# Layer 0's attention by joined head pairs: two of three pairs take all sixteen score groups first, then their values, and every row sum goes through DRAM

## The chip, the cores and the metric

The kernel runs on one core of one Trainium2 chip, as one launch. The metric is the device time of that launch in microseconds, lower is better. A core has a matrix engine (TensorE, PE in the profile), a vector engine (VectorE, DVE), a scalar engine for activations and copies (ScalarE, ACT), GpSimd (POOL), and SyncE (SP), which here only issues transfers. Each takes its instructions in the order in which the program holds them.

## The reference, cut to what matters

Eight images of 32 x 32 pixels with 384 channels pass through two layers in float32. Layer 0, the one that is changed, is a group norm and then attention with relative positions over all 1024 pixels of an image, six heads of 64 channels:

```python
qkv = x.reshape(b, hw, c) @ qkv_w + qkv_b                 # hw = 1024, c = 384
attn = jnp.einsum('bqd,bkd->bqk', q * SCALE, k)           # 1024 x 1024 per head
attn = attn + rel_h[..., :, None] + rel_w[..., None, :]   # from q and tables of offsets
out = jnp.einsum('bqk,bkd->bqd', jax.nn.softmax(attn), v)
x = x + out @ proj_w + proj_b
```

Layer 1 is a layer norm, causal attention with one head of 384, added to its input, and a second layer norm with a feed-forward of 1536 whose weights are binarized and whose activations are quantized in groups of one image; its groups cover the first five images, for the last three it yields zero. So images 0 to 4 run the feed-forward, 5 to 7 don't.

## The kernel before, in words

One program text is run over the images in the order 5, 0, 1, 2, 3, 4, 6, 7 (`ORDER`). Image 5, the first, also carries the preparation of weights in its attention and has some branches of its own ("image one"). The path described is the fast one, `f`. Its softmax has no maximum taken off; at the end a flag says whether a sum went out of bounds, and if so a second, general path `g` runs everything again behind a branch.

Within an image: products make queries, keys and values (L578), the tables of relative positions are spread through DRAM (`spread`, L769, and `place`, L784 to L800), then come layer 0's attention (`attend0_fast`, L888), the projection (L1021, L524) added to the residual (L1029), the layer norm's statistics (L481 to L489) and the normed tokens `f_xn` (L494), their transposes on TensorE (`f_pt`, L431) with ScalarE's copies out (L432), the split forms for the next products (L588), layer 1's attention (L1199, L1213) and, for five images, the feed-forward (L1357, L1407), beside which the next image's group norm is prepared.

The attention goes over three pairs of heads (`p`), and within each over two halves of 512 queries (`half`):

- `scores(p, c, half)` for eight blocks `c` of 128 keys: two matmuls of keys by queries (L904), two that add the position rows from `r` (L908), one pair each for the two heads of the pair, which lie on the two halves of the partitions; then two exponentials on ScalarE (L915) into a page. A page is a 128 x 1024 tile of float32; there are twelve. [...]
- `add_up`: VectorE adds the eight pages (L920 once, L922 six times).
- `values`: sixteen matmuls (L930), two for each page, into one PSUM bank; ScalarE copies the result to `oT` (L1002).
- `over_tiles`: a transpose in blocks (L939) and a reduction (L941) fold the sum to `few`, 128 x 32.
- `gathered`: SP puts `few` to DRAM (L949) and gets it back in four pieces as `parts` (L953), so that each partition holds the sums of its own queries. `reciprocals` adds these up (L969) and inverts (L971); `widened` copies them wide (L978) and transposes (L979); POOL multiplies `oT` by it (L999). This is done a half later, behind that half's sixth add.
- The last half of an image (`last`) goes another way: its `few` goes through two small matmuls with a fold matrix (L964) instead, and VectorE multiplies both of the last pair's halves (L1012, L1015) in front of the projection.

`later(p + 1)` is called in the first half of a pair and makes the next pair's rows of positions: ScalarE rounds (L784), VectorE subtracts (L794), and sixteen transfers, eight issued by SP and eight by POOL, place them (L800). `residual` loads the image again (L122) and POOL adds the projection's bias to it (L883, eight instructions).

A scheduler keeps each engine's order close to the program's text. Where a helper named `behind_of` or `issue_after` is used, the instruction is held behind a named other one; on TensorE the whole chain of matmuls of the attention is written out that way (`last_matmul`). Pools give out tiles in turn: a page, or one of ten image-sized rooms (`image`, `flat`), is handed out again when its last reader is done.

The projection begins with its first four blocks of tokens in this order, so that the third head pair's part (k = 2) comes as late as possible:

```python
for j, ks in ((0, (0, 1)), (1, (0, 1)), (0, (2,)), (1, (2,)), (2, (0, 1, 2)), (3, (0, 1, 2))):
```

At the end, the last image's layer 1 attention holds one block back, judges the sums (L282 to L291) and adds; SP writes the last outputs (L1525), and every engine loads the flag (L1539) and branches on it (L1540).

## Time and profile before

| what | us |
|---|---|
| three runs of the kernel before | 2262.17, 2261.61, 2261.36 |
| their median | 2261.61 |
| the profiled execution's own time | 2262.38 |
| its span in the profile | 2260.7 |
| TensorE busy | 2251.2 |
| VectorE busy | 1613.0 |
| ScalarE busy | 1208.5 |
| POOL busy | 526.9 |
| L904, L908 and L930 on TensorE, layer 0's attention | 399.0 + 307.7 + 340.2 |
| L920 and L922, VectorE's adds | 63.6 + 366.6 |

The profiled execution takes 2262.38 us, of which 2260.7 are the span from the first to the last instruction, and it is 0.8 us over the median of the three plain runs. The granted clock of TensorE was 0.999 throughout. A line of a timeline gives the start in microseconds from the span's beginning, the duration, the engine, the line of the kernel, the operation, what it writes and reads, and how many were merged into the line; in square brackets stands the idle time of the engine just ahead, and what ended it. A float32 matmul shows as two records. Busy time is added up without overlaps. `DVEq` and `SPq` are the queues in front of an engine.

### The profile page before, as it was taken

The numbers are of one execution on the slowest core, as the hardware profiler recorded it, in microseconds if no ns is written. First come the engines' busy times: TensorE is split into PE (matmuls) and PEld (weight loads), VectorE is DVE, ScalarE is ACT, GpSimd is POOL, SyncE is SP. The second block draws the span as 40 slices with busy tenths as digits, with TensorE's granted clock in tenths as the row PEclk, the third lists the DMA queues.
The fourth block names the chain that finished last, engine by engine and source line by source line (L and its number), as shares of the span: only waits on it lengthen the run. The fifth ranks groups of instructions, "written<-read, shape, count | busy, mean of one in ns | idle before, by whom it ended". The sixth has DMA issues, their size and how long they took to land.

```text
span 2260.7 us, 30149 instructions
## 1 busy us (share of the span) xinstructions
PE 2251.2 (100%) x10597; PEld 1380.3 (61%) x10597; DVE 1613.0 (71%) x2746; ACT 1208.5 (53%) x2181; POOL 526.9 (23%) x696
## 2 busy tenths in 40 slices
PE   9999999999999999999999999999999999999998
PEld 4547554768546677547685475874477754755475
DVE  6888578876788548886468884578854778727882
ACT  4654266337664457654477543767444766317541
POOL 7513231230231301313102313013040131221310
PEclk9999999999999999999999999999999999999999
DMA  7520562130730205520318203064102382016200
GB/s 188 158 86 29 162 138 68 49 148 29 155 100 29 84 29 126 129 58 1 112 39 189 56 29 112 24 148 112 30 9 104 71 173 64 7 47 155 55 1 30
DMA packets 182049, 188.50 MB, mean 83 GB/s; under 512 B 138764, under 2 KB 151489, under 8 KB 179073
## 3 DMA queue, kind: packets, MB, share of 16 engines
q1 hardware_dynamic: 163680, 115.80, 21.1%
q0 software_dynamic: 17376, 69.30, 9.8%
q8 instruction: 87, 1.43, 0.3%
q10 hardware_dynamic: 832, 1.38, 0.2%
q14 instruction: 74, 0.60, 0.1%
HBM read 84.52 MB, written 51.56 MB: 60 GB/s over the span
## 4 chain that ended last, share of the span: by engine, by line
PE 99%; DMA 0%; DVE 0%; SPq 0%; issue 0%
PE f_s L904 15%; PE f_av L930 15%; PE f_av L1213 8%; PE f_s L1199 8%; PE f_y L1407 7%; PE f_y L1357 7%; PE f_qk L578 6%; PE f_s L908 4%; PE f_pr_A L578 4%; PE f_pr_B L578 3%; PE f_pj L1021 3%; PE f_pj L524 3%; PE f_rel L578 2%; PE f_pr_1v_A L578 2%; PE f_pr_1q_A L578 2%; PE f_pr_1v_B L578 2%
## 5 line engine op out<-in xcount | busy, mean ns | idle before, releaser
L915 ACT ACTIVATE f_pr<-f_s 128x512 f32<-128x512 f32 x768 | 412.5, 595 | 41.8 <-PE f_s L908 37.1
L904 PE MATMUL f_s<-f_q,f_k 64*128 64x512 f32 x1536 | 399.0, 595 | 0.0
L922 DVE TENSOR_TENSOR f_sum<-f_sum,f_pr 128x1024 f32<-128x1024 f32 x288 | 366.6, 1273 | 25.9
L930 PE MATMUL f_av<-f_pr,f_v 128*64 128x512 f32 x1536 | 340.2, 595 | 0.0
L908 PE MATMUL f_s<-f_r,unit 64*128 64x512 f32 x768 | 307.7, 792 | 0.0
L930 PEld LDWEIGHTS f_av<-f_pr,f_v 128*64 128x64 f32 x1536 | 106.0, 137 | 218.2 <-issue 191.9
L904 PEld LDWEIGHTS f_s<-f_q,f_k 64*128 64x128 f32 x1536 | 145.6, 186 | 124.4 <-issue 66.2
L1199 PE MATMUL f_s<-f_q,f_lnT 128*128 128x512 f32 (+3 forms) x576 | 198.3, 488 | 0.0
L1213 PE MATMUL f_av<-f_v,f_pr 128*128 128x385 f32 (+1 forms) x576 | 195.4, 486 | 0.0
L800 POOL DMA_DIRECT2D f_r<-f_far x192 | 102.0, 534 | 382.0 <-DVE f_far L794 174.4
L1208 ACT ACTIVATE f_pr<-f_s 128x512 f32<-128x512 f32 (+3 forms) x96 | 47.0, 490 | 203.2 <-DVE f_s L1204 160.3
L1213 PEld LDWEIGHTS f_av<-f_v,f_pr 128*128 128x128 f32 x576 | 108.1, 190 | 77.0 <-issue 11.5
L1199 PEld LDWEIGHTS f_s<-f_q,f_lnT 128*128 128x128 f32 x576 | 100.7, 190 | 70.0 <-issue 46.9
L1368 DVE TENSOR_REDUCE am<-f_h 128x1 f32<-128x1024 f32 (+2 forms) x80 | 71.6, 946 | 95.6 <-ACT f_h L1361 95.6
L1361 ACT ACTIVATE f_h<-f_y,biases 128x256 f32<-128x256 f32 x240 | 100.6, 470 | 67.0 <-PE f_y L1357 67.0
L908 PEld LDWEIGHTS f_s<-f_r,unit 64*128 64x128 f32 x768 | 75.0, 187 | 89.9 <-issue 89.4
L578 PE MATMUL f_qk<-f_gnT,wq_sb 128*128 128x512 f32 x288 | 127.9, 595 | 0.0
L1407 PE MATMUL f_y<-f_w2a,f_hilo 128*128 128x384 f32 x640 | 127.2, 341 | 0.0
L1002 ACT COPY f_oT<-f_av 128x512 f32<-128x512 f32 x40 | 23.4, 585 | 190.2 <-PE f_av L930 190.2
L920 DVE TENSOR_TENSOR f_sum<-f_pr,f_pr 128x1024 f32<-128x1024 f32 x48 | 63.6, 1325 | 73.5 <-ACT f_pr L915 73.5
L1407 PEld LDWEIGHTS f_y<-f_w2a,f_hilo 128*128 128x128 f32 x640 | 112.6, 188 | 3.8 <-issue 1.4
L1311 POOL PARTITION_ALL_REDUCE qa<-qg x10 | 3.7, 365 | 459.1 <-DVE qg L1309 459.1
(286 smaller groups left out, 4154.4 us busy)
## 6 DMA issues: line engine op xcount, KB each, us to landing
f_far<-f_far SPq DMA_DIRECT2D x48, 512.0 KB, 5.3
f_r<-f_far SPq DMA_DIRECT2D x192, 128.0 KB, 3.3
f_r<-f_far POOLq DMA_DIRECT2D x192, 128.0 KB, 4.5
f_far<-f_far SPq DMA_DIRECT2D x192, 64.0 KB, 4.6
f_x<-in_x SPq DMA_DIRECT2D x32, 384.0 KB, 4.9
f_gnT<-in_xT SPq DMA_DIRECT2D x21, 512.0 KB, 4.7
f_w1a<-w1s POOLq DMA_DIRECT2D x5, 1536.0 KB, 6.7
f_w2a<-w2s POOLq DMA_DIRECT2D x5, 1536.0 KB, 7.3
```

Of the source, the lines that this page charges most:

```text
L578: last_product[0] = nc.tensor.matmul(*args, **kw).ins
L800: put = (nc.gpsimd if i else nc.sync).dma_start(out=r(part, p).bitcast(F32).rearrange("(m i) t -> i m t", i=4)[2 * i + d], in_=pages[i][ts ...
L904: nc.tensor.matmul(sc[par], k[rows[par], p, ts(c, P)], q[rows[par], p, ts(half, 512)], start=True, stop=False)
L908: last_matmul[0] = nc.tensor.matmul(sc[par], unit[rows[par], c // 2 % 2].rearrange("i h w -> i (h w)"), r(2 * (c // 4) + c % 2, p)[rows[pa ...
L915: last_exp[0] = nc.scalar.activation(pr[:, ts(par, 512)], sc[par], AF.Exp).ins
L922: adds.append(nc.vector.tensor_tensor(total, total, pr, ALU.add).ins)
L930: last_matmul[0] = nc.tensor.matmul(av[ts(par, HD), :], v[:, c, ts(2 * p + par, HD)], pr[:, ts(par, 512)], start=(c == 0), stop=(c == NJ - 1),
L1199: last_score[0] = nc.tensor.matmul(sc[:, lo:], xT[:, c // 4, k, ts(c % 4, P)], q[:, half, k, lo:], start=(k == 0), stop=(k == NC - 1),).ins
L1213: made = nc.tensor.matmul(av, prs[c][:, ts(j - c, P)], what(c), start=(c == 0), stop=(c == j)).ins
L1357: nc.tensor.matmul(ps, w1k[i // 2][:, ts(m, P)], xs[i % 2][:, half, i // 2, :], start=(i == 0), stop=(i == 2 * NC - 1))
L1361: nc.scalar.activation(pairs[i][:, m, :, :], ps[:, ts(i % 2, 256)].rearrange("p (j q) -> p j q", j=2), AF.Identity, bias=b1_sb[:, m : m + 1],)
L1407: nc.tensor.matmul(ps[:, :C], h, w, start=(i == 0), stop=(i == len(products) - 1))
```

## The change

All images but the first now use a new function, `by_pairs`. In it pairs 0 and 2 are joined: all sixteen score groups of a pair come first, both halves', and then the values of both halves, one after the other. For that the exponentials of six of the first half's eight key blocks go to two image-sized rooms instead of pages. Pair 1 still goes half by half. Every row sum of these images goes through DRAM, the last half's too; the fold matmuls are gone from them, and VectorE's two multiplications in front of the projection both wait for sums that come back. The reciprocals that wait are finished inside the next pair (`finish_waiting`, behind named adds). In a joined pair the next pair's rows of positions are made after the adds of both halves, and `over_tiles` and `gathered` of both halves follow after that. `rest_of` only returns what was returned before. The first image keeps the old loop.

At the end of the program the flag is loaded to registers (`values_load`) just before the very last addition instead of after everything, and the last of the output transfers is issued by ScalarE instead of SP.

In the kernel after, the lines are numbered differently: L904, L908, L915, L920, L922 and L930 become L902, L906, L913, L918, L920 and L928; L939, L941, L949, L953, L964 and L969 become L937, L939, L947, L951, L962 and L967; the multiplication on POOL is L989, ScalarE's copy of the values L995, VectorE's two last multiplications are L1034, the projection L1040 and L525, its addition L1051, the transposes L432, `f_xn` L495, the position rows L785, L795 and L801.

```diff
-            def scores(p, c, half):
+            def scores(p, c, half, pr=None):
...
-                pr = pools.page(f"pr0_{b}_{p}_{c}_{half}")
+                pr = pools.page(f"pr0_{b}_{p}_{c}_{half}") if pr is None else pr
...
+            def by_pairs():
+                oT, xt, waiting = None, None, []
+
+                def finish_waiting(adds, ats):
+                    for at, (p, half, few, parts) in zip(ats, waiting):
+                        with behind_of(adds[at]):
+                            rb = widened(p, half, reciprocals(p, half, few, parts))
+                        t = ts(half, 512)
+                        nc.gpsimd.tensor_tensor(oT[:, p, t], oT[:, p, t], rb, ALU.mult)
+                    waiting.clear()
+
+                def values_of(p, half, prs):
+                    av = values(p, half, prs)
+                    if (p, half) != (NPAIR - 1, 1):
+                        nc.scalar.copy(oT[:, p, ts(half, 512)], av)
+                    return av
+
+                def fold_up(p, half, total, ins):
+                    with behind_of(ins):
+                        few = over_tiles(p, half, total)
+                    waiting.append((p, half, few, gathered(p, half, few)))
+
+                for p in range(NPAIR):
+                    if p == 1:
+                        for half in range(2):
+                            prs = [scores(p, c, half) for c in range(NJ)]
+                            total, adds = add_up(p, half, prs)
+                            finish_waiting(adds, (5,) if half else (3, 5))
+                            values_of(p, half, prs)
+                            if not half:
+                                xt = residual()
+                                later(p + 1, last_exp[0], adds[-1])
+                            fold_up(p, half, total, adds[-1])
+                        continue
+                    rooms = [pools.flat(f"pr0_{b}_{p}_{i}") for i in range(2)]
+                    prs = [[scores(p, c, 0, rooms[(c - 2) // 3][:, ts((c - 2) % 3, T)] if c > 1 else None) for c in range(NJ)]]
+                    sums = [add_up(p, 0, prs[0])]
+                    finish_waiting(sums[0][1], (3,))
+                    prs.append([scores(p, c, 1) for c in range(NJ)])
+                    with behind_of(sums[0][1][-1]):
+                        sums.append(add_up(p, 1, prs[1]))
+                    if oT is None:
+                        oT = pools.image(f"oT_{b}")
+                    for half in range(2):
+                        av = values_of(p, half, prs[half])
+                    if p + 1 < NPAIR:
+                        later(p + 1, last_exp[0], sums[1][1][-1])
+                    for half in range(2):
+                        fold_up(p, half, sums[half][0], last_few[0] if half else sums[1][1][-1])
+                with behind_of(last_few[0]):
+                    for p, half, few, parts in waiting:
+                        t = ts(half, 512)
+                        rb = widened(p, half, reciprocals(p, half, few, parts))
+                        nc.vector.tensor_tensor(oT[:, p, t], av if half else oT[:, p, t], rb, ALU.mult)
...
+            if b != ORDER[0]:
+                return rest_of(*by_pairs())
...
                     products(av[:, :C], j, (j,), lambda c: v[:, c, :C])
+                failed.append(nc.values_load(flag[0:1, 0:1], min_val=0, max_val=P))
                 add(j, av)
...
-                        (nc.gpsimd if b in AFTER else nc.sync).dma_start(
+                        (nc.gpsimd if b in AFTER else nc.scalar if j == js[-2] else nc.sync).dma_start(
...
-    failed = nc.values_load(flag[0:1, 0:1], min_val=0, max_val=P)
-    with tc.If(failed > 0), ExitStack() as scope:
+    with tc.If(failed[0] > 0), ExitStack() as scope:
```

More of the change, by code (lines that the diff above doesn't have):

```diff
@@ L276, in conv_attn_hybrid @@
     flag = const.tile([1, 1], I32, name="flag")
+    failed = []
     def judge_sums(pools):
@@ L888, in attend0_fast @@
         def attend0_fast(residual, b, q, k, r, v, later):
-            oT = pools.image(f"oT_{b}")
             rows = (slice(0, HD), slice(HD, P))
@@ L980, in widened @@
                 return rb
+            def by_pairs():
[48 more added lines that the diff above has]
+                        nc.vector.tensor_tensor(oT[:, p, t], av if half else oT[:, p, t], rb, ALU.mult)
+                with behind_last():
+                    begun = {j: pools.o_tile(f"pj_{b}_{j}")[:, :C] for j in range(4)}
+                    for j, ks in ((0, (0, 1)), (1, (0, 1)), (0, (2,)), (1, (2,)), (2, (0, 1, 2)), (3, (0, 1, 2))):
+                        for i in ks:
+                            with tc.issue_after(last_matmul[0]):
+                                last_matmul[0] = nc.tensor.matmul(
+                                    begun[j], oT[:, i, ts(j, P)], wproj_sb[:, i, :], start=(i == 0), stop=(i == NC - 1)
+                                ).ins
+                return xt, oT, begun
@@ L982, in attend0_fast, with rest_of, begin, more @@
+            def rest_of(xt, oT, begun):
+                def begin(j):
+                    begun[j] = project(wproj_sb, slice(0, C), oT, j, f"pj_{b}_{j}")
+                def more(j):
+                    nc.vector.tensor_tensor(xt[:, j, :], begun[j], xt[:, j, :], ALU.add)
+                return xt, (begin, more)
+            if b != ORDER[0]:
+                return rest_of(*by_pairs())
+            oT = pools.image(f"oT_{b}")
             xt, waiting = None, None
@@ L985, in attend0_fast @@
                 prs = [scores(p, c, half) for c in range(NJ)]
-                if b == ORDER[0] and (p, half) == (0, 0):
+                if (p, half) == (0, 0):
                     with tc.issue_after(last_row[0]):
                         layer1_forms(pools, raw1[0], 1)
-                if b == ORDER[0] and (p, half) == (2, 0):
+                if (p, half) == (2, 0):
                     signs.append(binarize(pools))
@@ L1007, in attend0_fast @@
                 few = over_tiles(p, half, total)
-                at_once = last or (b == ORDER[0] and p == NPAIR - 1)
+                at_once = last or p == NPAIR - 1
                 if last:
@@ L1023, in attend0_fast @@
                             ).ins
-            def begin(j):
-                begun[j] = project(wproj_sb, slice(0, C), oT, j, f"pj_{b}_{j}")
-            def more(j):
-                nc.vector.tensor_tensor(xt[:, j, :], begun[j], xt[:, j, :], ALU.add)
-            return xt, (begin, more)
+            return rest_of(xt, oT, begun)
         def attend0_general(residual, b, q, k, r, v, later):
```

## The prediction

> **What bounds the kernel now.** I read the page's busy times and the chain first, then the waits, then the timelines of one image's attention (image 1, from 606 us) engine by engine. The page:

> ```profile
> PE 2251.2 (100%) x10597; PEld 1380.3 (61%) x10597; DVE 1613.0 (71%) x2746; ACT 1208.5 (53%) x2181; POOL 526.9 (23%) x696
> ...
> PE 99%; DMA 0%; DVE 0%; SPq 0%; issue 0%
> ```

> TensorE is never out of work and 99% of the chain is TensorE; its waits for others come to 2 us in all, at the start. So a gain must shorten TensorE's own stream, and a loss comes from any new wait of TensorE. TensorE's timeline (start, us, line):

> ```profile
> 614.05 1.02 PE L904 MATMUL f_s<-f_q,f_k 64*128 64x512 f32 x4
> ...
> 615.23 7.09 PE L930 MATMUL f_av<-f_pr,f_v 128*64 128x512 f32 x32
> 622.25 1.13 PE L904 MATMUL f_s<-f_q,f_k 64*128 64x512 f32 x4
> ...
> 623.45 1.02 PE L904 MATMUL f_s<-f_q,f_k 64*128 64x512 f32 x4
> ...
> 694.97 7.09 PE L930 MATMUL f_av<-f_pr,f_v 128*64 128x512 f32 x32
> 701.88 0.24 PE L964 MATMUL f_den<-few,fold 128*64 128x16 f32 x4
> 702.06 2.20 PE L1021 MATMUL f_pj<-wproj_sb,f_oT 128*128 128x384 f32 x6
> ...
> 713.77 1.47 PE L431 MATMUL f_pt<-ident,f_xn 128*128 128x128 f32 x12
> ...
> 725.88 1.67 PE L431 MATMUL f_pt<-ident,f_xn 128*128 128x128 f32 x12
> ```

> A score group recurs every 1.09 us, but the one before values takes 1.18 and the one after 1.20 (622.25 to 623.45). VectorE in the same image:

> ```profile
> 643.65 7.43 DVE L922 TENSOR_TENSOR f_sum<-f_sum,f_pr 128x1024 f32<-128x1024 f32 x5
> ...
> 670.73 1.18 DVE L941 TENSOR_REDUCE few<-f_tr 128x32 f32<-128x1024 f32 x1
> ...
> 675.00 6.54 DVE L922 TENSOR_TENSOR f_sum<-f_sum,f_pr 128x1024 f32<-128x1024 f32 x5
> ...
> 689.63 1.23 DVE L920 TENSOR_TENSOR f_sum<-f_pr,f_pr 128x1024 f32<-128x1024 f32 x1 [3.21 <-ACT f_pr L915]
> ...
> 704.92 0.69 DVE L1015 TENSOR_TENSOR f_oT<-f_av,f_wide 128x512 f32<-128x512 f32 x1
> ...
> 710.10 0.56 DVE L1029 TENSOR_TENSOR f_x<-f_pj,f_x 128x384 f32<-128x384 f32 x1 [0.57 <-PE f_pj L1021]
> ...
> 711.51 0.17 DVE L485 TENSOR_SCALAR lsd<-lmv 128x4 f32<-128x4 f32 x1
> ...
> 725.51 1.10 DVE L494 TENSOR_SCALAR f_xn<-f_x,lmv,lrs 128x384 f32<-128x384 f32 x2
> ```

> Before each half VectorE waits 1.1 to 3.2 us for the first exponentials, so a half's lateness dies there. After the projection begins (702.06) it waits only 0.73 us, for the third and fourth projection; from 713.7 to 736 its timeline shows no idle time of note. At 725.88 the second set of transposes takes 1.67 us against 1.47 at 713.77: the last of them already waits for the last f_xn, which ends at 726.61. So **from the projection to the second transposes there is no slack between VectorE and TensorE**, in any of the eight images. POOL's multiplications and SP's row-sum gather:

> ```profile
> 642.42 2.25 POOL L999 TENSOR_TENSOR f_oT<-f_oT,f_wide 128x512 f32<-128x512 f32 x1
> ...
> 670.97 1.26 POOL L999 TENSOR_TENSOR f_oT<-f_oT,f_wide 128x512 f32<-128x512 f32 x1 [9.52 <-DVE f_wide L979]
> ```
> ```profile
> 686.45 0.34 SPq L949 DMA_DIRECT2D f_few<-few  x1
> 687.89 1.73 SPq L953 DMA_DIRECT2D parts<-f_few  x4
> ```

> **What is removed.** Joining pairs 0 and 2 takes two scores-values-scores round trips out of each of seven images. A half's period is 622.25 - 606.30 = 15.95; eight steady groups take 8.73 and sixteen steady value pairs (0.429 from start to start) 6.86, so a round trip costs 0.35 (0.31 if only the long groups and the 0.11 of 7.02 against 6.91, values to L964, are counted). 14 x 0.35 = **-4.9**. The fold matmuls of the last half hold 0.175 us (701.88 to 702.06), of which values to projection may keep what values to scores costs, 0.11: 0.07 to 0.175, I take 0.1, x 7 = **-0.7**. The tail: SP's last output goes out at 2254.03 and the span ends at 2260.7; in between the engines load the flag and branch (SP sits 2255.34 to 2258.42 in its branch, VectorE 2254.30 to 2258.41), then end together. SP's load now comes earlier and the last output moves to ACT, which was ready earlier; VectorE's and POOL's ends stay (POOL's last drain ended at 2258.95, SP's chain at 2259.84). Between 0 and 1.7, I take **-0.9**. Together -6.5.

> **What is moved.** ACT's exponentials take 1.084 a group against 1.09 on TensorE, so sixteen in a row keep up. Pages and image rooms that ACT and VectorE wait for are freed over 6 us early. SP's seven more puts and 28 more gets (0.43 each) fit its idle queue; the next image's load slips some 14 us behind them and is not wanted for much longer. Pair 1's position tables now start after both halves of pair 0 are added up: 14 adds of 1.292 from 3.6 us give 21.8 us after pair 0's first score, the two L794 (3.16) 24.9, POOL's eight L800 (0.527 each) 23.4 to 28.7. With the median landing of 4.5 the first score's tables are there at 29.5; it reads them at 31.5 + 0.56 = 32.1. Cost nothing, cover 2.6 us; a landing over 7 us breaks it.

> **VectorE's backlog.** Times here run from the first score of the half or pair. Before, pair 1's first few is ready at 659.26 - 638.20 = 21.06. Now that half also carries a second reciprocal chain (L969 to L979: 0.19, 0.17, 0.2, 0.44, 0.6, so 1.6), POOL's eight residual adds moved beside its adds (1.45 an add beside one against 1.29, some five of them: 0.8) and a second multiplication beside two-input work. What that costs is in the rows: five adds take 7.43 beside an L999 and 6.54 alone, 0.89, and about 0.2 more on the add ahead: 1.1; or 0 beside transposes and reduces, as at 670.97. I take half, 0.5. 21.06 + 2.9 = 24.0 (22.7 to 25.5). The second half then follows without idle time, 12.65 (659.26 to 671.91): few at 36.65, which is 4.8 after pair 2's first score (31.87 after pair 1's) where it was 1.8. In pair 2 follow 14 adds (18.1), a chain (1.6), a multiplication that now falls beside adds (1.1) and transpose with reduce (2.4): few(2,0) at **28.0** (26.3 to 29.5).

> [...]

> **The projection.** Pair 2's values now end, and the projection begins, at 702.06 - 670.07 - 0.45 = 31.54. The row sums go to DRAM and back: put at once, first get 1.44 later (686.45 to 687.89), last get 1.30 after it, landing 1.8: 4.6 (5.2 by the one den that sat waiting, at 942.12, 2.43 after its last get). So pair 2's first sums are there at 28.0 + 4.6 = 32.6, **1.06 after the projection's start** (-0.6 to 3.2). From there to the finished oT: den, reciprocal, checks, copy, transpose and multiplication, 2.5 by their starts at 703.65 to 705.61; 3.55. TensorE can run four projections (0.653 each, 2.61) without it and starts some 0.35 after its releaser (726.61 to 726.99): a wait of 1.3. The first projection is then there at 2.61 + 1.3 + 0.65 + 0.2 = 4.75. Before, the first add L1029 began at 3.53 and L485 came 5.92 later at 9.45, 0.73 of it idle. Now half 1's chain stands between (2.3): 5.2 + 2.3 less 0.5 where neighbours fill the gaps of dependent pairs, 7.0. L485 comes at 11.75, **2.3 late**. Nothing behind it has slack, so by the second transposes TensorE has lost all 2.3: x 7 = **+16.1** (floor: no first wait, L485 at 3.48 + 7.0, 1.0 late, +7.2; ceiling: sums 3.2 after the start, 4.4 late, +31).

> [...]

> **Sum.** 16.1 - 6.5 = +9.6 on the profiled execution's 2262.4 (span 2260.7 and 1.7 around it), which is 0.8 above the median of 2261.6: **2271**. Lags of 1.7 to 3.2 give 2267 to 2278.

> **Rivals.** (A) Faster: the lateness at the projection is hidden and the saved switches stay. For it: 12 us of projections and transposes lie between L485 and the second transposes. Against: VectorE shows no idle time there. Price -6.5, 2255; it decides once the lag is under 0.93 an image (6.5/7). (B) The backlog is smaller than booked, the first wait vanishes and the lag is its floor, 1.0 to 1.7: +0.5 to +5.4, 2262 to 2267, no change that shows. For it: before, VectorE was idle 1.1 to 3.2 us ahead of every half. Against: pair 2's first half has no such idle time left. (C) Pair 1's tables come late as well: landings through POOL reach 10.3 us in places; from 7 us on each microsecond costs 7 over the images. For it: 2.6 us of cover where there were over 8. Against: in this window they took 2.4 to 5.9. With the forecast's lag, or with the ceiling's: 2278 to 2290. Should the switches not be won, each case is 4.9 later; the even 0.35 of every round trip speaks against it.

> **Chances and range.** Forecast 0.47, A 0.15, B 0.20, C 0.18. A measurement of this kernel tells about 0.2%, 4.5 us, from no change: below 2257.1 is A alone, 0.15; within is B, 0.20; slower 0.65. The range takes in most of A and C: 2256 to 2283.

> **What would show it.** After: scores of sixteen groups without a break and no matmul on L962; few(2,0) some 28 us after pair 2's first score; TensorE waiting about 1.3 at the third input of the first projection for the multiplication behind parts, then at the second transposes for f_xn, 2 us an image more than before; pair 1's first score without a wait; SP idle before the end. It is wrong if TensorE stays unbroken there, if the parts land before the values end, or if waits appear at pair 1's scores.

## The result

| kernel | median us | ratio to before, 95% interval |
|---|---|---|
| before | 2261.69 | 1 |
| after | 2290.44 (2289.53 to 2292.89) | 1.0129 [1.0111, 1.0146] |

The change costs 28.7 us where 9.6 were forecast; the sign was right, the size was three times the forecast and above the range's end of 2283. The profiled execution took 2292.89 us, span 2291.2, 30.5 more than the span before.

### The profile page after: what moved, and what is told of

Same layout as the page of the kernel before. It is cut to its first block, busy times and chain, and to the rows that moved or that the text cites. A ratio compares the mean times of both kernels' runs of the same rounds, so it can differ in the third digit from the quotient of the medians.

```text
span 2291.2 us, 30112 instructions
## 1 busy us (share of the span) xinstructions
PE 2258.0 (99%) x10569; PEld 1386.8 (61%) x10569; DVE 1645.3 (72%) x2753; ACT 1209.1 (53%) x2181; POOL 563.8 (25%) x696
## 3 DMA queue, kind: packets, MB, share of 16 engines
q8 instruction: 86, 1.41, 0.3%
## 4 chain that ended last, share of the span: by engine, by line
PE 81%; DVE 11%; DMA 4%; issue 2%; SPq 1%; ACT 1%; DVEq 0%; ACTq 0%
PE f_s L902 9%; PE f_av L1285 8%; PE f_s L1271 8%; PE f_y L1480 7%; PE f_y L1430 7%; PE f_av L928 6%; PE f_qk L579 5%; DVE f_sum L920 5%; PE f_pr_A L579 4%; PE f_pr_B L579 3%; PE f_pj L525 3%; PE f_s L906 2%; PE f_pj L1040 2%; PE f_rel L579 2%; PE f_pr_1v_A L579 2%
## 5 line engine op out<-in xcount | busy, mean ns | idle before, releaser
L913 ACT ACTIVATE f_pr<-f_s 128x512 f32<-128x512 f32 x768 | 413.3, 595 | 32.0 <-PE f_s L906 27.5
L920 DVE TENSOR_TENSOR f_sum<-f_sum,f_pr 128x1024 f32<-128x1024 f32 x288 | 388.3, 1348 | 26.2 <-ACT f_pr L913 0.5
L902 PE MATMUL f_s<-f_q,f_k 64*128 64x512 f32 x1536 | 398.0, 593 | 0.0
L928 PE MATMUL f_av<-f_pr,f_v 128*64 128x512 f32 x1536 | 337.1, 594 | 0.0
L906 PE MATMUL f_s<-f_r,unit 64*128 64x512 f32 x768 | 308.3, 792 | 0.0
L928 PEld LDWEIGHTS f_av<-f_pr,f_v 128*64 128x64 f32 x1536 | 107.2, 137 | 218.4 <-issue 199.9
L902 PEld LDWEIGHTS f_s<-f_q,f_k 64*128 64x128 f32 x1536 | 147.8, 186 | 115.9 <-ACT f_pr L913 57.7
L801 POOL DMA_DIRECT2D f_r<-f_far x192 | 102.0, 534 | 380.1 <-DVE f_far L795 276.2
L1285 PEld LDWEIGHTS f_av<-f_v,f_pr 128*128 128x128 f32 x576 | 108.1, 190 | 77.0 <-issue 11.5
L906 PEld LDWEIGHTS f_s<-f_r,unit 64*128 64x128 f32 x768 | 75.5, 187 | 89.4 <-issue 89.1
L884 POOL TENSOR_TENSOR f_x<-f_x,pb 128x384 f32<-128x384 f32 x64 | 109.1, 1738 | 49.0 <-DMA f_x<-in_x 31.7
L488 ACT ACTIVATE lsd<-lsd 128x4 f32<-128x4 f32 x26 | 5.4, 206 | 203.3 <-DVE lsd L486 203.3
```

Of the source, the lines that this page charges most:

```text
L801: put = (nc.gpsimd if i else nc.sync).dma_start(out=r(part, p).bitcast(F32).rearrange("(m i) t -> i m t", i=4)[2 * i + d], in_=pages[i][ts ...
L884: nc.gpsimd.tensor_tensor(xt[:, j, :], xt[:, j, :], pb, ALU.add)
L902: nc.tensor.matmul(sc[par], k[rows[par], p, ts(c, P)], q[rows[par], p, ts(half, 512)], start=True, stop=False)
L906: last_matmul[0] = nc.tensor.matmul(sc[par], unit[rows[par], c // 2 % 2].rearrange("i h w -> i (h w)"), r(2 * (c // 4) + c % 2, p)[rows[pa ...
L913: last_exp[0] = nc.scalar.activation(pr[:, ts(par, 512)], sc[par], AF.Exp).ins
L920: adds.append(nc.vector.tensor_tensor(total, total, pr, ALU.add).ins)
```

## The profile after

The page: TensorE's busy time hardly moves, the chain that ended last does. VectorE and transfers now hold a sixth of it.

```profile
PE 2258.0 (99%) x10569; PEld 1386.8 (61%) x10569; DVE 1645.3 (72%) x2753; ACT 1209.1 (53%) x2181; POOL 563.8 (25%) x696
...
PE 81%; DVE 11%; DMA 4%; issue 2%; SPq 1%; ACT 1%; DVEq 0%; ACTq 0%
```

The waits of TensorE (engine, line, tile, who it waited for: us in total, times, longest). Before, the first line was not there:

```profile
PE f_pj L1040 <- DVE f_oT L1034: 24.9, 7, 3.8
PE f_zeros L404 <- DVE f_zeros L402: 1.5, 1, 1.5
```

So TensorE waits in each of the seven images at the one place that the prediction named, for the multiplication that follows the gather. TensorE's timeline at image 1's projection:

```profile
705.55 2.85 PE L1040 MATMUL f_pj<-wproj_sb,f_oT 128*128 128x384 f32 x8
711.68 7.12 PE L1040 MATMUL f_pj<-wproj_sb,f_oT 128*128 128x384 f32 x16 [3.28 <-DVE f_oT L1034]
718.64 4.03 PE L525 MATMUL f_pj<-wproj_sb,f_oT 128*128 128x384 f32 x12
722.51 1.47 PE L432 MATMUL f_pt<-ident,f_xn 128*128 128x128 f32 x12
```

The wait is 3.28 us, and the sixteen matmul records behind it then take 7.12 us. In image 2 the same sixteen take 5.43:

```profile
1021.53 5.43 PE L1040 MATMUL f_pj<-wproj_sb,f_oT 128*128 128x384 f32 x16 [3.04 <-DVE f_oT L1034]
```

The difference is the clock. Stretches of 3.41 us across the wait of image 1, and the one that ends in the wait of image 2 (us; busy time of PE, PEld, DVE, ACT and POOL; then PEclk, the share of the full clock that TensorE was granted, and the share and GB/s of the DMA engines):

```profile
709.14:712.55 3.41, 0.87 (x3) 0.61 (x4) 2.32 (x7) 0.00 (x0) 0.00 (x0) 1.00 0.28 37
712.55:715.96 3.41, 3.41 (x7) 1.78 (x6) 3.06 (x11) 0.00 (x0) 0.00 (x0) 0.50 0.96 363
715.96:719.38 3.42, 3.42 (x12) 2.00 (x11) 2.48 (x5) 0.00 (x0) 0.00 (x0) 1.00 0.17 71
...
1019.75:1023.16 3.41, 1.63 (x5) 1.06 (x6) 2.25 (x5) 0.00 (x0) 0.00 (x0) 1.00 0.42 75
```

After the stretch in which TensorE was busy for 0.87 us of 3.41 it ran one stretch at half clock, 0.50. This happened in six of the seven images, in the last one for two stretches; image 2, where TensorE was busy for 1.63 us of the stretch, kept the full clock. The mean clock fell from 0.999 to 0.994. Nothing of this was in the prediction.

Why the gather is so late stands in VectorE's and POOL's timelines of pair 1 and pair 2 (image 1):

```profile
645.81 1.22 DVE L918 TENSOR_TENSOR f_sum<-f_pr,f_pr 128x1024 f32<-128x1024 f32 x1 [5.17 <-ACT f_pr L913]
647.14 5.72 DVE L920 TENSOR_TENSOR f_sum<-f_sum,f_pr 128x1024 f32<-128x1024 f32 x3
...
654.91 1.84 DVE L920 TENSOR_TENSOR f_sum<-f_sum,f_pr 128x1024 f32<-128x1024 f32 x1
...
681.06 1.48 DVE L918 TENSOR_TENSOR f_sum<-f_pr,f_pr 128x1024 f32<-128x1024 f32 x1
...
703.22 1.22 DVE L939 TENSOR_REDUCE few<-f_tr 128x32 f32<-128x1024 f32 x1
...
709.01 0.26 DVE L967 TENSOR_REDUCE den<-parts 128x16 f32<-128x64 f32 x1 [2.17 <-DMA parts<-f_few]
```
```profile
644.92 14.63 POOL L884 TENSOR_TENSOR f_x<-f_x,pb 128x384 f32<-128x384 f32 x8 [5.25 <-DMA f_x<-in_x]
```

Before, in the same image, the bias additions began 5.5 us ahead of pair 1's first score and were done by 642.46; of pair 1's adds only the first ran beside them:

```profile
632.70 9.76 POOL L883 TENSOR_TENSOR f_x<-f_x,pb 128x384 f32<-128x384 f32 x8 [0.85 <-DMA f_x<-in_x]
```

Now POOL's eight bias additions take 14.63 us: seven of them run beside VectorE's adds and take 1.98 each instead of 0.99, and six adds take 1.84 instead of 1.23. Pair 1's first few comes 26.3 us after its first score. From there VectorE goes through pair 1's second half and both halves of pair 2 without idle time ahead of any (681.06 is pair 2's first add), so the lateness stays. Pair 2's first few comes at 704.44, 30.4 after that pair's first score (30.3 to 30.9 in the seven images); the parts land 4.57 later, 3.5 after the projection's start.

The whole difference can be added up from the two traces. How much later the last of the second transposes starts, counted from the projection's first matmul (25.21 before): 5.72, 5.18, 3.25, 5.59, 5.40, 5.54 and 6.63, in sum **+37.3**. From an image's first score to its projection: 95.72 before and 94.95 after on average, in sum over seven images **-5.5**. From the end of VectorE's last addition to the end of the span: 6.66 before, 5.75 after, **-0.9**. That makes +30.9 of the 30.5; the first image's attention, for one, began 0.6 earlier.

## The experiments

Two things stood side by side in each image: VectorE's lateness and the half clock. The experiments ask what each costs, what makes VectorE late (the bias additions, the way through DRAM, or the joining), and which of the two joined pairs it takes.

### Four blocks of the projection first

```diff
-for j, ks in ((0, (0, 1)), (1, (0, 1)), (0, (2,)), (1, (2,)), (2, (0, 1, 2)), (3, (0, 1, 2))):
+for j, ks in ((0, (0, 1)), (1, (0, 1)), (2, (0, 1)), (3, (0, 1)), (0, (2,)), (1, (2,)), (2, (2,)), (3, (2,))):
```

> The kernel after, with the projection's first four blocks taking all their parts of pairs 0 and 1 before any part of pair 2: eight matmul steps (5.2 us) instead of four (2.6) lie ahead of the wait for the multiplication that follows the gather. Theory (VectorE's chain is late by itself, and the half clock that follows TensorE's long wait costs some 2 us more in six of seven images): the wait shrinks from about 3.6 to 1 us, no half-clock window appears, VectorE's chain is as late as before, so the second transposes stay 3.3 late an image: about 2279. Rival 1 (only TensorE's own wait counts): 2.6 x 7 less, 2272. Rival 2 (the half clock is a bystander and VectorE sets all of it): 2288 to 2290.

Measured: 2281.1 (2279.1 to 2282.6), ratio 1.0087 [1.0070, 1.0104]. The clock stays at 1.0 from the first image on (mean 1.0). In the profiled execution pair 2's parts land 3.8 us after the projection's start on average (3.7 in the kernel after), so VectorE is just as late, and the last transposes are 3.3 late an image where they were 5.3. The spans differ by 13.8 us, the medians by 9.3. TensorE's waits (as above):

```profile
PE f_pj L1040 <- DVE f_oT L1034: 7.2, 7, 2.3
PE f_pt L432 <- DVE f_xn L495: 6.4, 7, 0.9
PE f_pj L525 <- DVE f_oT L1034: 4.2, 7, 0.6
```

The half clock goes and VectorE's lateness stays, as the theory had it. But the 13.8 us are not the half clock alone, since the order also gives TensorE real work to do in the wait. In each of the seven images the last transposes come late by 0.45 less than the parts land after the projection's start (5.0 and 4.6 in image 0, say). In image 2 of the kernel after, which had no half clock either, they come late by 0.03 more than that. So the order itself saves 0.5 an image, 3.4 in all.

### The wait filled with matmuls that do nothing

The result of the added matmuls is not used; all else is the kernel after.

```diff
-for j, ks in (..., (1, (0, 1)), (0, (2,)), ...):
+spare = pools.o_tile(f"spare_{b}")[:, :C]
+for j, ks in (..., (1, (0, 1)), (None, range(4)), (0, (2,)), ...):
+    if j is None: nc.tensor.matmul(spare, oT[:, 0, ts(i, P)], wproj_sb[:, 0, :], ...)
```

> The kernel after, with four idle-filling matmuls (128x384, 0.65 us each, their result is not used) on TensorE between the projection's first four steps and the wait for pair 2's part. They lie inside the wait of 3.3 to 3.8 us and move nothing else. Theory (the half clock that follows the wait is a cost of its own): what is left of the wait, about 1 us, is too short for a half-clock window; the transposes come 3.3 late instead of 5.3, 9 to 14 us less over the run: 2277 to 2281. Rival (the half clock hides under VectorE's own lateness): 2288 to 2292, unchanged.

Measured: 2284.8 (2283.7 to 2286.4), ratio 1.0102 [1.0085, 1.0119]. TensorE's timeline at image 1's projection:

```profile
704.85 2.85 PE L1046 MATMUL f_pj<-wproj_sb,f_oT 128*128 128x384 f32 x8
707.53 2.74 PE L1042 MATMUL f_spare<-wproj_sb,f_oT 128*128 128x384 f32 x8
711.59 5.43 PE L1046 MATMUL f_pj<-wproj_sb,f_oT 128*128 128x384 f32 x16 [1.31 <-DVE f_oT L1034]
```

The records behind the wait take 5.43 again, no stretch runs at half clock (mean 0.999), and the kernel gets faster by doing 18 us of useless work. By less than expected, though: 5.6 by the medians, 8.0 by the spans. In this execution the parts landed 4.1 us after the projection's start instead of 3.7, which is some 3 us of the difference. So the half clock has a price of its own. In all seven images the last transposes now come late by what the parts land after the projection's start, and 0.03 to 0.04 more. In the kernel after it is 0.03 more in image 2, which had no half clock, 1.6 to 1.7 more where one stretch ran at half clock, and 2.6 more where two did: **11.0 us** in all in its profiled execution, which is what the 8.0 and the 2.8 of the later parts make. In the plain runs, where the landing isn't seen, only the 5.6 are measured.

### POOL's bias additions held back

They wait for pair 2's last sum and then run beside VectorE's transposes and reductions.

```diff
-xt = residual()
+xt = residual(bias=False)                                   # loads only
...
+if p == NPAIR - 1:
+    gate = pools.small.tile([P, 1], F32, tag="gate", name=f"gate_{b}")
+    total = sums[1][0]
+    opened = nc.gpsimd.tensor_tensor(gate, total[:, 0:1], total[:, 0:1], ALU.add).ins
+    with tc.issue_after(opened):
+        residual(xt, True)                                  # the eight additions
```

> The kernel after, with POOL's eight additions of the projection's bias held back until pair 2's last sum is there, so that they no longer run beside pair 1's adds. Theory (these additions are what made VectorE 3.7 us later than I had booked): the first few of pair 2 comes 26.8 us after its first score instead of 30.5, the parts land at about the projection's start, TensorE's wait falls to 0 to 0.5, no half-clock window, the second transposes are 1.0 to 1.3 late: 2262 to 2265. Rival (the way through DRAM costs it whatever VectorE does): the wait stays over 2 us, 2280 or more.

Measured: **2257.34** (2256.33 to 2258.51), ratio 0.9980 [0.9970, 0.9990]. It is faster than both kernels, and some 5 us faster than the theory had it. VectorE, POOL and TensorE in image 1, and TensorE's wait over the whole run:

```profile
641.88 3.88 DVE L920 TENSOR_TENSOR f_sum<-f_sum,f_pr 128x1024 f32<-128x1024 f32 x3
...
672.39 1.23 DVE L918 TENSOR_TENSOR f_sum<-f_pr,f_pr 128x1024 f32<-128x1024 f32 x1 [1.02 <-ACT f_pr L913]
...
694.30 1.22 DVE L939 TENSOR_REDUCE few<-f_tr 128x32 f32<-128x1024 f32 x1
```
```profile
693.35 7.73 POOL L884 TENSOR_TENSOR f_x<-f_x,pb 128x384 f32<-128x384 f32 x8
```
```profile
700.29 8.07 PE L1046 MATMUL f_pj<-wproj_sb,f_oT 128*128 128x384 f32 x24
```
```profile
PE f_pj L1046 <- DVE f_oT L1040: 0.9, 2, 0.6
```

The same three adds take 3.88 instead of 5.72, the additions 7.73 instead of 14.63. Pair 1's first few is at 21.8 after its first score instead of 26.3, VectorE has caught up by pair 2's first add (it waits 1.02 us for it), and pair 2's first few is at 26.75 instead of 30.4. The parts land at the projection's start (-0.3 to 0.8), and TensorE waits 0.9 us there in all, in two images. The transposes are 0.0 to 0.8 late, where the theory still had 1.0 to 1.3. In one image (3) TensorE stops in pair 1's first scores at a matmul that reads the position rows, and pair 1 goes on 1.1 late; the trace names no releaser, but one of those rows' transfers took 8.5 us to land, against 5.7 at most in image 1 of the kernel after.

### Pair 2's sums by matmuls on TensorE

```diff
-waiting.append((p, half, few, gathered(p, half, few)))
+waiting.append((p, half, few, gathered(p, half, few) if p < NPAIR - 1 else None))
...
+# den of half 0 ahead of the projection, den of half 1 behind its first four steps
```

> The kernel after, with pair 2's two sums folded by small matmuls on TensorE as before instead of going through DRAM; pairs 0 and 1 still go through DRAM and the bias additions stay where they are. Theory (the 4.6 us of the gather lie on the path): the first few of pair 2 still at 30.5, the multiplication ends 3.3 after the projection's start instead of 5.3 to 6, a wait of about 1 us, no half-clock window, lag 1.3: about 2264. Rival (the backlog of VectorE is all that matters): the wait stays near 3, 2285 or more.

Measured: 2263.5 (2262.0 to 2265.7), ratio 1.0008 [0.9998, 1.0017]: 27 us less than the kernel after, and no difference from before that can be told. TensorE's wait at the projection:

```profile
PE f_pj L1035 <- DVE f_oT L1048: 2.6, 4, 1.1
```

Pair 2's first few is as late as ever (29.7 to 31.1), but its multiplication ends 2.7 to 4.1 after the projection's start instead of 5.8 to 6.6, no stretch inside the run is at half clock (mean 0.999), and the transposes are 0.4 to 1.5 late.

### Both

> Both edits: bias additions late and pair 2's sums by matmuls on TensorE. Theory: first few of pair 2 at 26.8, 4.7 before the projection, no wait of TensorE and no lag at the transposes, so what joining saves is left: 14 x 0.35 for the switches, and 0.9 at the end: about 2256. Rival (something else in the joined order is late too, or POOL's additions now delay the projection's sums): 2262 or more.

Measured: 2258.8 (2258.6 to 2259.6), ratio 0.9987 [0.9977, 0.9997], so no better than the late additions alone, and 2.8 above the theory. The trace says why: no wait of TensorE is left, but the matmuls of the sums lie in its stream again, one of them between the projection's steps, and the transposes are an even 0.36 late in each image, 2.5 us in all.

### One pair joined

```diff
# pair 0 only
-if p == 1:
+if p != 0:
# pair 2 only
-if p == 1:
+if p != 2:
```

with the next pair's rows and the image's load where the loop over halves had them in the pair that isn't joined.

> The kernel after with only pair 2 joined; pair 0 goes half by half, and position rows, image load and bias additions come where they came before. Theory: few of pair 1's second half about 2 us after pair 2's first score, pair 2's first few at 26.8, its parts at the projection's start, no wait or one of 0.5: about 2258. Rival (the joined last pair with its gather at the projection is what costs, whatever came before): 2275 or more.

Measured: 2259.9 (2259.2 to 2260.7), ratio 0.9991 [0.9982, 1.0000]. This is 2 us above the theory, and far from the rival. The bias additions lie where they lay before and take 9.88 us, pair 2's first few comes at 26.75, and TensorE's waits at the projection are short:

```profile
PE f_pj L1043 <- DVE f_oT L1037: 0.9, 2, 0.7
```

In three images the transposes are 0.3 to 0.9 late, in the others not at all.

> The kernel after with only pair 0 joined; pair 2 goes half by half like pair 1, its sums through DRAM. Theory (joining pair 0 moves the bias additions beside pair 1's adds, but the lateness only costs where pair 2 is joined as well and its first half has no room left): few of pair 1's second half still about 7 us after pair 2's first score, caught up in pair 2's first half, pair 2's first sums finished long before the projection, no wait of TensorE there. Left are 7 x 0.35 for the switches, 0.7 for the folds and 0.9 at the end: about 2258. Rival (joining pair 0 is what costs): 2275 or more.

Measured: 2269.2 (2268.9 to 2270.7), ratio 1.0033 [1.0021, 1.0044]. Neither the theory nor the rival. Pair 2's first sums were indeed done before the projection, but VectorE and TensorE show another wait (image 1):

```profile
710.86 0.56 DVE L482 BATCH_NORM_STATS2 lst<-f_x 128x6 f32<-128x384 f32 x1
711.46 0.18 DVE L483 BATCH_NORM_AGGREGATE lmv<-lst 128x2 f32<-128x6 f32 x1
711.63 0.27 DVE L967 TENSOR_REDUCE den<-parts 128x16 f32<-128x64 f32 x1
```
```profile
702.23 8.01 PE L1040 MATMUL f_pj<-wproj_sb,f_oT 128*128 128x384 f32 x24
710.07 2.74 PE L525 MATMUL f_pj<-wproj_sb,f_oT 128*128 128x384 f32 x8
714.25 1.56 PE L525 MATMUL f_pj<-wproj_sb,f_oT 128*128 128x384 f32 x4 [1.44 <-DVE f_oT L1034]
```

VectorE's order has the last half's den behind the fourth projection's addition and statistics; it starts without a wait at 711.63, 5 us after its last get was issued, and the multiplication comes too late for the projection's second four blocks. The transposes are 1.65 late in every image, 11.5 us; less what is won, 4, that is the 7.1 measured. So an experiment that should have isolated one cost met another: where on VectorE the last sum is put.

### The late additions and four blocks first

Both edits shown above together.

> Bias additions late and the four-block order of the projection. With the additions late alone, two of seven images still showed TensorE waiting 0.4 to 0.8 us at the projection, and the transposes came 0 to 0.8 late. Theory: those waits go, 2256 to 2257. Rival (the second transposes are set by VectorE, which the order doesn't help): the same as with the additions late alone, 2257.3.

Measured: 2270.6 (2270.5 to 2271.7), ratio 1.0040 [1.0026, 1.0053]: 13 us worse than the late additions alone, which neither the theory nor the rival had. VectorE in image 1:

```profile
704.12 0.69 DVE L1040 TENSOR_TENSOR f_oT<-f_oT,f_wide 128x512 f32<-128x512 f32 x1
708.40 0.56 DVE L1057 TENSOR_TENSOR f_x<-f_pj,f_x 128x384 f32<-128x384 f32 x1 [3.59 <-PE f_pj L1046]
```

The multiplication is in time, but with eight steps ahead of it the first finished projection comes 6.2 us after the start instead of 3.7, VectorE idles 3.59 us for it, L486 comes at 12.4 instead of 10.1 and the transposes are 2.1 late, 14.7 over seven images. The order that helps a TensorE that waits anyway harms one that doesn't.

### The end of the program alone

```diff
 # the kernel before, with
+failed.append(nc.values_load(flag[0:1, 0:1], min_val=0, max_val=P))   # ahead of the last addition
-nc.sync.dma_start(out=dst...)
+(nc.scalar if j == js[-2] else nc.sync).dma_start(out=dst...)
```

> The kernel before with the change's last part alone: the flag loaded before the last addition and the last output issued by ScalarE. Theory: from the end of VectorE's last addition to the end of the span 5.8 us instead of 6.7, so 2261.0. Rival (VectorE's or POOL's end sets it anyway): 2261.9.

Measured: 2261.68 (2261.46 to 2263.84) beside 2262.03, ratio 0.9999 [0.9990, 1.0008]; no difference that can be told. In the profiled execution 6.11 us pass from the end of VectorE's last addition to the end of the span, between the 6.66 of before and the 5.75 of after.

## Why the prediction was wrong in size

**What held.** What joining saves: 5.5 measured against 4.9 and 0.7. The end: 0.9 in the trace, though alone it made no difference that could be told. Pair 1's first scores after a joined pair 0 came without a wait in the kernel after (31.5 us from pair 0's first score in every image), so the tables' cover of 2.6 us held there. The steps from few to parts, 4.57 against 4.6, and from den to the multiplication's end, 2.61 against 2.5. VectorE's 23.2 us from pair 1's last few to pair 2's first: 23.3. And the place: TensorE waits at the third input of the first projection, seven times.

**The step that failed first** is the term "some five of them: 0.8" for the bias additions beside pair 1's adds. They cost 4.5: pair 1's first few is at 26.3 with them and at 21.8 without (the late additions). I had priced an add beside one at 1.45, which fits rows where only some adds are covered (six in 8.48 us at 627.18 before, 1.41 each). An add that is covered wholly takes 1.84, and those same six hold one, at 633.83, beside additions of 1.88 and 1.97. Slower adds keep POOL's additions slow too, at 1.98 instead of 0.99, so seven of the eight run beside them and not five. Six adds at 1.84 are 3.7 of the 4.5. All else that changed in that half was booked at 2.1, for a second chain and half a multiplication, and came to 0.7 net. So pair 1's first few was at 26.3, not 24.0, and pair 2's at 30.4, not 28.0 and beyond the 29.5 that I had as its end. Over the seven images the parts landed 3.73 after the projection's start on average, not 1.06.

**The step that was missing** is the half clock. A wait of TensorE was priced at its length. In the kernel after, waits of 3.3 to 3.8 us are followed by a stretch of 3.41 us at half clock, 1.6 to 1.7 us more an image, and 2.6 in the last, which has two. In its profiled execution that makes 11.0 us. With the forecast's wait of 1.3 it would probably not have come: with the wait filled, six images waited 1.1 to 1.4 us and one 2.2, and none ran at half clock.

**"Nothing behind it has slack"** was too strong. In the kernel with late additions L486 comes at 10.09 where it came at 9.45, and the last transposes at 25.22 where they came at 25.21: 0.6 us is absorbed. The floor of rival B, 1.0 an image, was in truth about 0. The prediction's steps make the transposes late by 1.24 more than the parts land after the projection's start (2.3 for 1.06). In the images of the kernel after, of the filled wait, of the late additions and of pair 2 alone joined in which the parts landed after that start and no half clock followed, they came late by just that landing and 0.03 to 0.05. So parts at 3.73 make 3.8 an image and not 4.9. This step erred on the other side and hid a part of the first error.

**A reading that was wrong.** VectorE did not wait 1.1 to 3.2 us before each half: in the kernel before, pair 1's second half begins without a wait in all seven images (659.18 in image 1). The sums of the prediction did count that half as following without idle time. What it left out is the other side: with the late additions VectorE still idles some 1.0 us ahead of pair 2, so a smaller lateness would have died there.

In sum the 16.1 that were forecast for seven images were 37.3 in the profiled execution: 18.7 more for the later parts (7 x 2.67), 11.0 more for the half clock, and 8.5 less for what follows the parts (7 x 1.21).

**The rivals.** A and B needed VectorE to be earlier than it was. With the bias additions out of the way the lag is near nothing, as A had it, and the time is 2257.3 where A had 2255; B's floor of 1.0 an image showed nowhere. C, a wait at pair 1's scores, did not happen in the kernel after; a stop that looks like it showed once, 1.1 us, in the kernel with late additions.

**What stays open.** The price of the half clock in a plain run; the two kernels without it are 5.6 and 9.3 faster by the medians, and each differs in one thing more. The kernel with late additions (2257.3) is still some 2 us above what the switches and the end would give; in its profiled execution three images are 0.5 to 1.1 us late, which is about that much. Another order of the last den on VectorE, which the kernel with pair 0 alone asks for, was not tried.

## What to carry to other kernels

Before moving work under another engine's shadow, price it with a row in which the two engines overlap wholly, and look at the times of both: here a POOL addition and a VectorE add beside each other took 1.98 and 1.84 instead of 0.99 and 1.23, and eight small additions, 8 us in all, decided a change that was about TensorE's order. A wait on the bounding engine may not be paid by its length alone: here six waits of 3.28 to 3.81 us brought 1.6 to 2.6 us more each at half clock. Ask what its clock does afterwards, and what the engine behind it was waiting to start with. When a change loses, look for the one piece that was moved along with it: holding back eight additions turned +28.7 us into -4.6.

## What the runs showed of the hardware

A VectorE add (L920) and a POOL bias addition (L884) beside each other took 1.84 and 1.98 us in image 1 of the kernel after, instead of 1.23 and 0.99. With the additions held back, all eight took 7.73 us beside VectorE's transposes and reductions, and the reduction at 694.30, beside them, took 1.22 as the one at 703.22 of the kernel after did without them.
